# A two-column copy of a selective scan, moved from behind a table load to a place among the SiLUs

## The chip, the cores and the metric

The kernel runs on one core of one Trainium2 chip. The metric is the device time of one execution in microseconds (us). The engines are named as in the profile: PE (matrix multiplication), PEld (its weight loads), DVE (vector engine), ACT (activation engine), POOL (GpSimd), SP (the queue that issues most DMAs).

## What is computed

Two layers run over 32 images of 128 channels and 56 x 56 pixels. Layer 0 is a 7 x 7 depthwise convolution, a layer norm and a mixture of eight experts. Layer 1, in which the change lies, is a 1 x 1 convolution, a 3 x 3 convolution branch with SiLU, and a selective scan (Mamba) over the 3136 pixels of each image:

```python
xz = t @ in_proj_w.T
xm, z = jnp.split(xz, 2, axis=-1)              # 256 channels each
xm = silu(causal_conv4(xm) + conv1d_b)
dt, Bm, Cm = jnp.split(xm @ x_proj_w.T, [8, 24], axis=-1)
dt = softplus(dt @ dt_proj_w.T + dt_proj_b)
dA = exp(dt[..., None] * A)                    # 16 states for each channel
dBu = dt[..., None] * Bm[:, :, None, :] * xm[..., None]
h = dA_t * h + dBu_t                           # for every pixel in order
y = einsum('bds,bs->bd', h, C_t)
y = y + xm * D
return y * silu(z) @ out_proj_w.T
```

## The kernel before

Layer 1 cuts each image into 7 chunks of 448 pixels (8 rows). A chunk is called a group here; there are 32 x 7 = 224 groups, and each has 16 states. Channels lie on the 128 partitions, and the 256 channels of the scan are two halves side by side, so that one instruction on both halves has 2 x 448 columns, or 2 x 449 with a leading column for each half.

A unit u is one state i of one group: u = 16 g + i. For each unit

- POOL multiplies `db = du * B` (`db_pool`, L1099), with B copied to all partitions by a DMA from a small DRAM tile (`bc_load`, L1093);
- ACT computes the decay `da = exp(dt * A)` in two instructions, one for each half (`exp_act`, L1105). There are two `da` buffers, in PSUM, used by even and odd units in turn;
- DVE runs the scan `h = da * h + db` over 898 columns (`scan_dve`, L1114). In the leading column of each half the decay is zero and `db` holds the value that the state had at the end of the previous group, so one scan carries on both halves. For the states 0, 4, 6, 7, 12 and 15 (`POOL_C`) the result goes to a tile `hs` of its own; for the other ten it goes over `da` itself;
- POOL (for those six states) or DVE (for the ten) multiplies `prod = h * C` (`cmul`, L1120);
- ACT copies the two last values of `h`, one for each half, into the leading columns of that state's `db` tile (`carry_act`, L1126). In the last group of an image it copies zeros instead. The copy is next needed by the same state's scan one group later; and the decay of the unit two further on overwrites the `da` that it reads;
- PE sums `prod` over the states into the PSUM tile `py` (`sum_pe`, L1059).

The order of every engine's instructions is written out by hand in the loop at the end of `layer1`: step t issues the loads of units t+8 and t+4, `yz` if it falls in this step, POOL's product of unit t-1, the copy of unit t-1, `db` of unit t+4, the decay of unit t+1, the scan of unit t and, for the ten states, its product, then the sums and the side work. The side work of a group (`at(offset, function)`) is spread over the steps before and after its states.

In step i = 2 of each group the side work holds `silus(g)` of the following group. It works on ACT with another table of functions than the exponentials. In order: the table load of the SiLUs (L930), the two `xm` SiLUs (L930), the `lt` SiLU of the group before (L943), the two `zs` SiLUs (L946), and the table load of the exp set (L947). PE's two `p_z` products (L936), which the `zs` SiLUs read, go into the PSUM buffers that the `xm` SiLUs have read. `px_pe` (L953) follows on PE, then the `py` sums of step 3 and, in step 4, `p_cvc` (L829), which `sq_act` (L856) reads on ACT. `yz` (L1051) on DVE falls in step 4.

ACT's order around the SiLUs before the change is therefore: decay of state 3, table load, `xm`, `xm`, `lt`, `zs`, `zs`, table load, copy of state 2, decay of state 4, copy of state 3, decay of state 5.

Of the kernel before, what the change touches and what calls it, by code (L numbers as in the profile page):

```python
# [27 lines left out]
DS = 16  # L28
# [6 lines left out]
CH1 = L // NQ1  # L35
TPC1 = CH1 // TT
POOL_C = (0, 4, 6, 7, 12, 15)
HD = 64

NB0 = 4  # L40
# [4 lines left out]
def tile_kernel(tc: tile.TileContext, a: dict, out: bass.AP):  # L45
# [14 lines left out]
    with (  # L60
# [414 lines left out]
        def weights(wp, wt, pw):  # L475
# [13 lines left out]
            def turned(v, t):  # L489

                for h in range(2):
                    nc.sync.dma_start(
                        out=t[h * HD : (h + 1) * HD],
                        in_=v[h * 128 : (h + 1) * 128].rearrange("(r d) k -> d r k", r=2),
# [31 lines left out]
            for k in range(2):  # L526
                for r in range(2):
                    for j, v in enumerate((bbi, bsc)):
                        nc.scalar.copy(bnt[k * HD : (k + 1) * HD, r, j : j + 1], v[r * HD : (r + 1) * HD, :])

# [220 lines left out]
        with tc.tile_pool(name="p3", bufs=2, space=PSUM) as pmm:  # L751

            def mm_tile(name):
                return pmm.tile([128, 512], F32, name=name, tag="mm")

            layer1(w3 | locals())
# [3 lines left out]
def layer1(s):  # L760
# [12 lines left out]
    with (  # L773
# [149 lines left out]
        def silus(g):  # L923

            if g < G:
                d = st[g]
                xm = d["xm"] = two.tile([128, 2, CH1], F32, name="xm")
                zs = d["zs"] = three.tile([128, 2, CH1], F32, name="zs")
                for h in range(2):
                    nc.scalar.activation(  # L930
                        xm[:, h, :], d.pop(f"p_xm{h}")[:, :CH1], AF.Silu, bias=s["c1b"][:, h : h + 1]
                    )
                ps = []
                for h in range(2):
                    p = mm_tile("p_z")
                    nc.tensor.matmul(  # L936
                        p[:, :CH1], lhsT=s["wz"][:, h * 128 : (h + 1) * 128], rhs=d["te"][:, DC - 1 :],
                        start=True, stop=True,
                    )
                    ps.append(p)  # L940
            if g > 0:
                lt = st[g - 1]["lt"]
                nc.scalar.activation(lt, lt, AF.Silu)  # L943
            if g < G:
                for h in range(2):
                    nc.scalar.activation(zs[:, h, :], ps[h][:, :CH1], AF.Silu, bias=s["zb"][:, h : h + 1])  # L946
            nc.scalar.preload_act_table_set("natural_log_exp_and_others")  # L947
# [71 lines left out]
        def lt_pe(g, ts):  # L1019
# [5 lines left out]
            for t in ts:  # L1025
                dy, dx = divmod(t, 3)
                for r in range(2):
                    rs = slice(r * HD, (r + 1) * HD)
                    for k in range(2):
                        nc.tensor.matmul(  # L1030
                            d["p_l"][r][k * HD : (k + 1) * HD, : CH1 // 2], lhsT=s["dwd"][rs, t, rs],
                            rhs=d["xh"][rs, dy + k * R : dy + (k + 1) * R, dx : dx + HW], start=t == 0, stop=t == 8,
                        )

        def lt_act(g, r):
# [3 lines left out]
            lt, p = d["lt"], d["p_l"][r]  # L1039
            rs = slice(r * HD, (r + 1) * HD)  # L1040
            for k in range(2):
                ks = slice(k * HD, (k + 1) * HD)
                nc.scalar.activation(
# [23 lines left out]
        def dd_pe(g):  # L1067
            d = st[g]
            d["py"] = pyp.tile([128, 2, 512], F32, name="py3")
            tiles(py(g), lambda rs, h: s["dd"][rs, h, rs], d["xm"], True, False)  # L1070
# [17 lines left out]
        def bc_load(u, which):  # L1088
            g, i = divmod(u, DS)
            if i % SB == 0:  # L1090
                t = three.tile([128, SB, CH1], F32, name=which)
                r = DR + i + (DS if which == "cb" else 0)
                nc.sync.dma_start(out=t, in_=st[g]["bc_d"][r : r + SB, :].partition_broadcast(128))  # L1093
                for k in range(SB):
                    units[u + k][which] = t[:, k, :].unsqueeze(1).to_broadcast([128, 2, CH1])

        def db_pool(u):
            g, i = divmod(u, DS)
            nc.gpsimd.tensor_tensor(dbv[i][:, :, 1:], st[g]["du"], units[u].pop("bb"), ALU.mult)  # L1099

        def exp_act(u):
            g, i = divmod(u, DS)
            da = das[u % 2]
            for h in range(2):
                nc.scalar.activation(  # L1105
                    da[:, h * W1 : (h + 1) * W1], st[g]["dt"][:, h, :], AF.Exp, scale=s["aneg"][:, h, i : i + 1]
                )

        def scan_dve(u):
            i = u % DS  # L1110
            w = units[u]
            da = das[u % 2]
            hs = three.tile([128, 2 * W1], F32, name="hs", bufs=2) if i in POOL_C else da
            nc.vector.tensor_tensor_scan(hs, da, dbs[i], 0.0, ALU.mult, ALU.add)  # L1114
            w["hs"] = hs.rearrange("p (h t) -> p h t", h=2)

        def cmul(u, eng):
            w = units[u]
            w["prod"] = three.tile([128, 2, CH1], F32, name="prod", bufs=5)
            eng.tensor_tensor(w["prod"], w["hs"][:, :, 1:], w.pop("cb"), ALU.mult)  # L1120

        def carry_act(u):
            g, i = divmod(u, DS)
            hs = units[u].pop("hs")
            last = zeros if g % NQ1 == NQ1 - 1 else hs[:, :, CH1]
            nc.scalar.copy(dbv[i][:, :, 0], last)  # L1126

        def sum_pe(u):
            g, i = divmod(u, DS)
            tiles(py(g), lambda rs, h: ident[rs, rs], units[u].pop("prod"), False, i == DS - 1)  # L1130
# [29 lines left out]
        at(-33, moe_act)  # L1160
        at(-16, xm_pe, 1)
        at(-14, silus)
        at(-14, px_pe)
        at(-29, cv1_pe, "p_cvc", "cv1c")
# [10 lines left out]
        at(-25, var_pe)  # L1175
        at(-9, sp_exp)
        work.setdefault(DS * G - 14, []).append((silus, G))

        def valid(u):
            return 0 <= u < U  # L1180

        with tc.manual_schedule():
            for t in range(-40, U + 24):
                i = t % DS

                if valid(t + 8):
                    bc_load(t + 8, "bb")
                if valid(t + 4):
                    bc_load(t + 4, "cb")
                side = work.pop(t, [])  # L1190
                for w in side:
                    if w[0] is yz_dve:
                        w[0](*w[1:])

                if valid(t - 1) and (t - 1) % DS in POOL_C:
                    cmul(t - 1, nc.gpsimd)
                if valid(t - 1):
                    carry_act(t - 1)
                if valid(t + 4):
                    db_pool(t + 4)  # L1200

                if valid(t + 1):
                    exp_act(t + 1)

                if valid(t):
                    scan_dve(t)
                    if i not in POOL_C:
                        cmul(t, nc.vector)

                if i == 3 and valid(t - 3):  # L1210
                    dd_pe((t - 3) // DS)
                if i % 2 == 1:
                    for u in (t - 3, t - 2):
                        if valid(u):
                            sum_pe(u)
                for w in side:
                    if w[0] is not yz_dve:
                        w[0](*w[1:])
# [35 lines left out]
```

## Time and profile before

| What | Value |
|---|---|
| Median of 3 runs | 16215.65 us (16211.88 to 16220.98) |
| The profiled execution | 16201.56 us |
| Its span, first to last instruction | 16199.8 us |
| Granted PE clock, mean over the span | 0.907 |
| Busy share of PE, PEld, DVE, ACT, POOL over the span | 79%, 43%, 68%, 66%, 84% |
| The same from 5750 to 16150 us (layer 1) | 90%, 41%, 93%, 85%, 95% |
| Table load (L930, L947), each | 1.283 us |
| Decay (L1105), one half | 0.639 us |
| Scan (L1114) | 2.02 us |
| Copy (L1126) from `da`, from `hs` | 0.162 us, 0.193 us |

A line of the timeline gives the start in us, the duration in us, the engine, the line of the kernel and the operation, output before input, with the number of instructions merged into it; in brackets stands the idle time before it and what ended it. A line of the costliest groups gives after the bar the busy time in us, the mean duration in ns, the idle time in front of these instructions and, with an arrow, what ended most of it. The busy shares are averages over stages; what bounds a stage is read from the waits in it.

### The profile page before, as it was taken

Reading aid. Unit: us, or ns where it says so; the run is one execution under the profiler, and the core shown is the slowest. Engines: PE = TensorE matmul, PEld = TensorE weight load, DVE = VectorE, ACT = ScalarE, POOL = GpSimd, SP = SyncE. Lnnn points to the kernel's source line nnn. Section 1 sums busy time; section 2 is a strip of 40 time slices with the busy share of each in tenths; the row PEclk is TensorE's granted clock in tenths of the full one; section 3 lists DMA queues with packets and bytes.
Section 4 is the critical chain, followed back from the end, with each engine's and each line's share of the span. In section 5 each row is a group of like instructions: output and inputs, shape, how many; then the busy total and the mean of one; then the engine's idle time right before and its main releaser. Section 6 shows DMA issues by size and latency. Waiting matters only on the chain. (4 is left out here: it accounts for less than half of the span.)

```text
span 16199.8 us, 246168 instructions
## 1 busy us (share of the span) xinstructions
PE 12759.5 (79%) x91637; PEld 7021.4 (43%) x91637; DVE 11083.8 (68%) x9909; ACT 10643.5 (66%) x20982; POOL 13611.7 (84%) x9017
## 2 busy tenths in 40 slices
PE   7996100006999989999999999899899999999988
PEld 7995100005777734444444444444444444444443
DVE  2656300001111179999999999999999999999999
ACT  4655100003444478888888888888888888888887
POOL 2443477777888889999999999999999999999999
PEclk9996555558999999999999999999999999999999
DMA  8785433334555555555555555555555555555555
GB/s 266 231 240 195 158 105 102 107 96 69 71 71 72 64 154 175 172 175 176 173 176 174 175 176 174 174 175 175 174 173 175 175 173 176 175 174 175 175 173 162
DMA packets 1239122, 2572.09 MB, mean 159 GB/s; under 512 B 139336, under 2 KB 676640, under 8 KB 1230240
## 3 DMA queue, kind: packets, MB, share of 16 engines
q1 hardware_dynamic: 1041440, 2361.89, 47.1%
q0 software_dynamic: 196480, 194.45, 7.0%
q8 instruction: 721, 11.81, 0.3%
q14 instruction: 481, 3.94, 0.1%
HBM read 2180.38 MB, written 375.43 MB: 158 GB/s over the span
## 5 line engine op out<-in xcount | busy, mean ns | idle before, releaser
L1099 POOL TENSOR_TENSOR db<-du,bb 128x896 f32<-128x896 f32 x3584 | 6847.2, 1934 | 17.6
L1105 ACT ACTIVATE da<-dt,aneg 128x449 f32<-128x449 f32 x7168 | 4577.3, 639 | 269.4 <-DVE prod L1120 86.7
L1114 DVE TENSOR_TENSOR_SCAN da<-da,db 128x898 f32<-128x898 f32 x2240 | 4523.0, 2019 | 2.8 <-ACT da L1105 2.5
L1059 PE MATMUL py<-prod,ident 64*64 64x448 f32 x28672 | 3100.6, 545 | 21.7 <-POOL prod L1120 15.5
L1114 DVE TENSOR_TENSOR_SCAN hs<-da,db 128x898 f32<-128x898 f32 x1344 | 2673.1, 2015 | 487.4 <-ACT db L1126 441.9
L1120 POOL TENSOR_TENSOR prod<-hs,cb 128x896 f32<-128x896 f32 x1344 | 2595.1, 1931 | 459.8 <-PE p_cvc L829 343.6
L1120 DVE TENSOR_TENSOR prod<-da,cb 128x896 f32<-128x896 f32 x2240 | 2446.2, 1092 | 217.6 <-issue 3.5
L744 ACT COPY xc<-ept 128x512 f32<-128x512 f32 (+1 forms) x248 | 143.8, 580 | 2738.9 <-PE ept L742 2738.9
L650 POOL DMA_INDIRECT buf_d<-xg,slot x1568 | 1516.3, 967 | 487.3 <-issue 477.1
L702 POOL DMA_INDIRECT res_d<-ys,xb x984 | 1591.7, 1618 | 333.1 <-issue 285.6
L1059 PEld LDWEIGHTS py<-prod,ident 64*64 64x64 f32 x28672 | 1042.4, 133 | 1446.2 <-issue 1176.9
L742 PE MATMUL ept<-ident,xb 128*128 128x128 f32 (+1 forms) x984 | 188.8, 274 | 1849.0 <-DMA xb<-buf_d 1849.0
L914 PE MATMUL p_xm<-te,wk 128*128 128x448 f32 x3584 | 1415.8, 546 | 1.0 <-DVE te L898 0.6
L694 DVE TENSOR_TENSOR ys<-py,b2t 128x512 f32<-128x512 f32 (+2 forms) x256 | 170.9, 670 | 1679.4 <-PE py L688 1662.6
L647 DVE COPY xg<-gate 128x28 f32<-128x28 f32 x56 | 11.7, 213 | 1746.4 <-DMA buf_d<-xg,slot 1746.4
L688 PEld LDWEIGHTS py<-w2t,hh 128*128 128x128 f32 x7872 | 936.5, 191 | 175.2 <-issue 113.1
L688 PE MATMUL py<-w2t,hh 128*128 128x128 f32 x7872 | 985.2, 278 | 0.2
L914 PEld LDWEIGHTS p_xm<-te,wk 128*128 128x128 f32 x3584 | 658.7, 189 | 730.8 <-issue 572.0
L179 PE MATMUL pc<-xc,toep 112*112 112x112 f32 (+1 forms) x8192 | 935.0, 270 | 35.2 <-ACT toep L168 31.1
L742 PEld LDWEIGHTS ept<-ident,xb 128*128 128x128 f32 (+1 forms) x984 | 124.6, 143 | 1852.7 <-issue 1852.6
L179 PEld LDWEIGHTS pc<-xc,toep 112*112 112x112 f32 x8192 | 878.5, 184 | 45.3 <-ACT toep L168 38.8
L936 PE MATMUL p_z<-te,wz 128*128 128x448 f32 x896 | 522.3, 717 | 466.3 <-ACT xm L930 466.3
(235 smaller groups left out, 19412.9 us busy)
## 6 DMA issues: line engine op xcount, KB each, us to landing
bb<-bc_d SPq DMA_DIRECT2D x1792, 448.0 KB
cb<-bc_d SPq DMA_DIRECT2D x1792, 448.0 KB
toep<-toep_d SPq DMA_DIRECT2D x448, 392.0 KB
xg<-res_d SPq DMA_DIRECT2D x56, 1792.0 KB
buf_d<-zero SPq DMA_DIRECT2D x28, 2275.0 KB
xb<-buf_d SPq DMA_DIRECT2D x240, 260.0 KB
xt<-in_x SPq DMA_DIRECT2D x32, 1568.0 KB
res_d<-xa SPq DMA_DIRECT2D x128, 392.0 KB
```

What stands on the lines that cost most here:

```text
L179: nc.tensor.matmul(pc[:, c, :, lo:hi], lhsT=tp[c // 2][:, c % 2, 6 - 2 * o : 8 - 2 * o, :], rhs=s4[:, c, :, lo + o - 1 : hi + o - 1], star ...
L650: apart(nc.gpsimd.indirect_dma_start(out=buf_d[:, :], out_offset=bass.IndirectOffsetOnAxis(ap=slots[k][:, o + j : o + j + 1], axis=0), in_ ...
L688: nc.tensor.matmul(py[:n, j, :], lhsT=hh[:, k, j * 128 : j * 128 + n], rhs=w2t[:, k, :], start=k == 0, stop=k == KF - 1,)
L702: apart(nc.gpsimd.indirect_dma_start(out=res_d[:, :], out_offset=bass.IndirectOffsetOnAxis(ap=xb[:n, j, C + 1 : C + 2].bitcast(I32), axis= ...
L742: nc.tensor.transpose(pt[:, j * 128 : j * 128 + n], xb[:n, j, :C], ident[:n, :n])
L914: nc.tensor.matmul(p[:, :CH1], lhsT=s["wk"][:, k, hs], rhs=d["te"][:, k : k + CH1], start=k == 0, stop=k == DC - 1 and not first,)
L936: nc.tensor.matmul(p[:, :CH1], lhsT=s["wz"][:, h * 128 : (h + 1) * 128], rhs=d["te"][:, DC - 1 :], start=True, stop=True,)
L1059: nc.tensor.matmul(ps[r][h * HD : (h + 1) * HD, :CH1], lhsT=lhsT(rs, h), rhs=rhs[rs, h, :], start=start, stop=stop,)
L1099: nc.gpsimd.tensor_tensor(dbv[i][:, :, 1:], st[g]["du"], units[u].pop("bb"), ALU.mult)
L1105: nc.scalar.activation(da[:, h * W1 : (h + 1) * W1], st[g]["dt"][:, h, :], AF.Exp, scale=s["aneg"][:, h, i : i + 1])
L1114: nc.vector.tensor_tensor_scan(hs, da, dbs[i], 0.0, ALU.mult, ALU.add)
L1120: eng.tensor_tensor(w["prod"], w["hs"][:, :, 1:], w.pop("cb"), ALU.mult)
```

## The change

The copy of state 2 is no longer issued at the start of step 3, behind the second table load, but inside `silus`, behind the two `xm` SiLUs and PE's `p_z` products and ahead of the `lt` SiLU. There `g` is the following group, so `g - 1` is the group whose scan is running. The copies of the other 15 states stay where they are. In the built program the number of instructions and of table loads is the same, the order on PE, DVE, POOL and SP is the same, and ACT's order differs in this copy alone, once in each of the 224 groups.

```diff
@@ -35,6 +35,7 @@
 CH1 = L // NQ1
 TPC1 = CH1 // TT
 POOL_C = (0, 4, 6, 7, 12, 15)
+CARRY = 2
 HD = 64
 
 NB0 = 4
@@ -939,6 +940,7 @@
                     )
                     ps.append(p)
             if g > 0:
+                carry_act(DS * (g - 1) + CARRY)
                 lt = st[g - 1]["lt"]
                 nc.scalar.activation(lt, lt, AF.Silu)
             if g < G:
@@ -1194,7 +1196,7 @@
 
                 if valid(t - 1) and (t - 1) % DS in POOL_C:
                     cmul(t - 1, nc.gpsimd)
-                if valid(t - 1):
+                if valid(t - 1) and i != CARRY + 1:
                     carry_act(t - 1)
                 if valid(t + 4):
                     db_pool(t + 4)
```

## The prediction

> **What bounds the kernel now.** I read the slices of the page first: from slice 15 of 40 on, the busy digits no longer change, so layer 1 is a steady loop. Its 224 groups fill about 10,400 us (224 x 46.61, the mean distance from one group's first table load to the next in the timeline). Then the costliest groups of instructions and the list of waits, to see which engine of the loop ever stands still:
>
> ```profile
> L1114 DVE TENSOR_TENSOR_SCAN hs<-da,db 128x898 f32<-128x898 f32 x1344 | 2673.1, 2015 | 487.4 <-ACT db L1126 441.9
> L1120 POOL TENSOR_TENSOR prod<-hs,cb 128x896 f32<-128x896 f32 x1344 | 2595.1, 1931 | 459.8 <-PE p_cvc L829 343.6
> ...
> L936 PE MATMUL p_z<-te,wz 128*128 128x448 f32 x896 | 522.3, 717 | 466.3 <-ACT xm L930 466.3
> ```
>
> The reader is to see 487 us of idle DVE in front of one kind of scan, 460 us of idle POOL in front of one kind of product: about 2 us a group each, and no other large hole on either. Where the hole lies, the timeline of one group shows, ACT first, then DVE, then POOL:
>
> ```profile
> 10036.98 1.28 ACT L930 ACT_TABLE_LOAD   x1
> 10038.27 1.16 ACT L930 ACTIVATE xm<-p_xm,c1b 128x448 f32<-128x448 f32 x2
> 10039.32 0.58 ACT L943 ACTIVATE lt<-lt 128x448 f32<-128x448 f32 x1
> 10040.02 0.64 ACT L946 ACTIVATE zs<-p_z,zb 128x448 f32<-128x448 f32 x1
> 10041.15 0.63 ACT L946 ACTIVATE zs<-p_z,zb 128x448 f32<-128x448 f32 x1 [0.49 <-PE p_z L936]
> 10041.80 1.28 ACT L947 ACT_TABLE_LOAD   x1
> 10043.09 0.16 ACT L1126 COPY db<-da 128x2 f32<-128x2 f32 x1
> 10043.28 1.31 ACT L1105 ACTIVATE da<-dt,aneg 128x449 f32<-128x449 f32 x2
> ```
> ```profile
> 10035.34 2.02 DVE L1114 TENSOR_TENSOR_SCAN da<-da,db 128x898 f32<-128x898 f32 x1
> ...
> 10041.60 1.08 DVE L1051 TENSOR_TENSOR yz<-py,zs 128x896 f32<-128x896 f32 x1
> 10044.70 2.03 DVE L1114 TENSOR_TENSOR_SCAN hs<-da,db 128x898 f32<-128x898 f32 x1 [2.02 <-ACT db L1126]
> ```
> ```profile
> 10046.86 1.92 POOL L1120 TENSOR_TENSOR prod<-hs,cb 128x896 f32<-128x896 f32 x1 [1.82 <-PE py L1059]
> ```
>
> The DVE is done with yz at 10042.68 and waits for the decay of state 4, which ends on ACT at 10044.59; the scan starts 0.1 later, and POOL's product of state 4 follows that scan. ("PE py" is only the last releaser by the profile; the scan's end at 10046.73 is what came 0.13 before.) ACT is late because five SiLUs lie between two table loads, and the copy of state 2 stands after the second load. So once a group the loop hangs on the chain: DVE product of state 1, decay of state 3, load, SiLUs, load, copy, decay of state 4, scan of state 4. All else in the group is DVE work back to back. A tenth saved on this chain is a tenth off the group, as long as the hole (1.3 us in the shortest groups, 3.2 in the longest) is larger than that.
>
> **What the skill says.** "ScalarE: Activation LUTs", section "Table sets: the hidden batching unit": cheap functions, copy among them, are filler in every set, so a copy among SiLUs needs no load. The trace of before runs these copies with the exp set alone, so it can't show it; the built program after the change still has two loads a group. "Perfetto Trace Analysis", section "Per-instruction lifecycle": ACT is strictly first in, first out, and a wait for a semaphore lies before the reported start. The trace agrees: the decay stands 0.19 behind the copy at 10043.09, with nothing between. "TensorE: Matmul & The Clock Gate", Part 1: the array's clock is halved by a free-running window of 4096 cycles (3.413 us) after idling. The trace agrees: the stretches that begin with the wait for xm have a granted clock of 0.79 in some groups and 1.00 in others, and sorting the 223 first loads by start time modulo 3.413 us sorts the blocks into short and long ones.
>
> **The change, part by part.** Nothing is added: 224 copies leave the place after the second load and stand behind the xm SiLUs. Only ACT's order changes; no DMA, no matmul and no instruction of SP or POOL moves.
>
> *Removed after the load.* Between the load's end and the copy lie 0.01 us. In 192 groups the copy reads da, and the decay of state 4 overwrites da, so it waits for the copy: 0.195 us from start to start in each. In the other 32 (last of an image) it copies zeros and the decay follows 0.098 after it. Afterwards the decay follows the load at once; the SiLU behind the first load starts 0.01 after it (10038.26 to 10038.27), so I take the whole distance: 192 x 0.195 + 32 x 0.098 = 40.6 us. Bound below: if the decay, whose scale is a pointer, needs 0.1 more after a load, 40.6 - 22 = 18 us; above there is no more to take.
>
> *Added among the SiLUs.* The copy needs the scan of state 2. That ends at 10037.36; its new place is reached about 10039.32, where lt starts now. So it is 1.96 us in hand and nothing queued behind it (lt, two zs, load, decay) waits for DVE. A copy whose successor doesn't wait for it costs 0.08 to 0.1 (the copy at 10047.94 and the decay at 10048.02). lt then starts at about 10039.41, zs could start at 10039.9, but zs starts at 10040.02 because p_z is ready only then, and the second zs at 10041.15, after 0.49 of waiting. The cover is PE's p_z, which hangs on the xm SiLUs ahead of the copy and is not moved. Cost taken: 0. If that cover were gone it would cost 0.1 x 224 = 22 us.
>
> *What is late next.* PE's row is not moved: p_z, p_x, the py sums and p_cvc still follow xm. Thus ACT's square (L856), which already waits for p_cvc in 108 groups, waits as much longer as ACT comes earlier, and the decays of states 6 and 7 behind it don't move. In the quoted group the square waited 0.92, and the scans of states 6 and 7 took 4.18 us together instead of 3.94. Going through the timeline, the scan of state 7 has no slack once that wait is 0.69 or more (27 groups), and 0.21 when it is under 0.5. Lost: 27 x 0.19 + 15 groups between x 0.1 = 6.6 us. Left: 34 us, bounds 12 and 41.
>
> *The clock window.* A group's length depends on where its first load lies in the 3.413 us window:
>
> ```profile
> core 0: us, PE busy (x) PEld busy (x) DVE busy (x) ACT busy (x) POOL busy (x), PEclk, DMA share, GB/s
> 9336.11:9382.17 46.06, 41.15 (x306) 19.15 (x306) 43.47 (x29) 39.67 (x81) 44.27 (x28) 1.00 0.57 176
> 9382.17:9429.49 47.32, 42.65 (x306) 19.43 (x306) 43.46 (x29) 39.67 (x81) 44.62 (x28) 0.96 0.55 173
> ```
>
> Two neighbouring groups with the same work: the second is 1.26 us longer at a lower clock. Load to load takes 4.44 us in 97 groups (mean group 46.06), over 5.2 in 87 (47.20). A group of 46.06 advances by 46.06 - 13 x 3.413 = 1.69, half a window, so two bring the loop back almost to the same place. Starts are bunched: 113 of 223 lie in the three eighths of the window around its turn. If all eighths were equally frequent, the mean of the eighths' means would be 46.54, not 46.61: 0.07 x 223 = 16 us. A group of 45.87 advances by 1.50 and spreads the starts more evenly; I take 15 us more gain, an estimate, with bounds of a gain of 40 and a loss of 25, since the bunching can turn out either way.
>
> *Sum.* 40.6 - 6.6 + 15 = 49 us. The profiled execution took 16201.56 (span 16199.8), which would become about 16152.5; it lies 14 below the median of the three runs, 16215.65. On that median the forecast is 16215.65 - 49 = 16166.
>
> **The rivals.** *The late square takes most of it back*: if every one of the 108 groups that wait for p_cvc loses its part, 116 x 0.18 = 21 us remain and the clock gives nothing: 16195. For it: the wait grows by construction. Against: state 7 has slack in most of them. *The change does nothing*: the copy lengthens the SiLU block by what it frees behind it. if it takes 0.18 there as on average after the load, 40.6 - 40.3 = about 0, 16216. Against it: the 0.49 and 0.12 of waiting in front of the zs. *Slower by the clock window*: the new step bunches the groups in the long part. A long group costs 47.20 - 46.06 = 1.14 more than a short one, so 34 gained us are eaten by 30 more long groups (87 to 117), and from 60 more it is slower beyond the measurement; 70 more give 16215.65 - 34 + 80 = 16262. For it: the present bunching shows that the step can lock. Against: the present one is near a half window, the new one is not near a simple fraction.
>
> **How the numbers follow.** The measurement can tell about 0.2% (32 us) from no change. Forecast 0.77, at 16166, its own range 16130 to 16183; square takes it back 0.11 (16195); does nothing 0.06 (16216); slower 0.06 (16262). Faster by over 0.2%: 0.77; within: 0.11 + 0.06 = 0.17; slower: 0.06. The range runs from 16130 (41 direct and 40 of clock are 81, little beyond it) up to 16200, which takes in the second case and leaves out the last two, 0.12, and tails.
>
> **What would show it.** After: no copy at L1126's new number between the second load and the decay; the decay 0.01 behind the load; zs starting as long after xm as now (1.75 us in a short group), and load to load still 4.44 in short groups; shortest groups 45.87 instead of 46.06; DVE's idle before hs down from 487 to about 450 us; ACT's wait for p_cvc up from 61.5 by some 20 to 30 us. Wrong if lt or zs start later than p_z allows, if the short groups stay at 46.06, or if the share of groups over 5.2 us from load to load rises above half.

## The result, and the profile after

Six runs of the changed kernel gave a median of 16164.69 us (16146.63 to 16166.55), six of the kernel before 16218.31 (16209.85 to 16236.96): a ratio of 0.9965, 95% interval 0.9954 to 0.9976, or 54 us (39 to 75 by the interval). The forecast was 16166. The profiled execution took 16164.69 (span 16163.0), so the two profiles lie only 37 us apart; layer 1 accounts for more than that, as the row of the decays, which gives their number, their shortest, median and longest duration in ns and the start of the first and the last, shows for each kernel:

```profile
L1105 ACT ACTIVATE da<-dt,aneg x7168: 629/639/648, 5740.1 to 16183.2; 128x449 f32<-128x449 f32 x200
```
```profile
L1107 ACT ACTIVATE da<-dt,aneg x7168: 629/639/649, 5750.6 to 16146.6; 128x449 f32<-128x449 f32 x200
```

From first to last decay it is 10443.1 before and 10396.0 after, 47 us less. Layer 0, which the change doesn't touch, happened to end 10.5 later in the second profile. This length of layer 1 is what I compare below, beside the ratios. It is read from one trace of each kernel; two traces of the changed kernel differ by 3.5 us (10396.0 and, in `after_again`, 10392.5), and with fillers two of one kernel agree (10274.4 in `e_after_dummy` and in `e_again`).

The page of the changed kernel, its costliest groups (all line numbers have moved by one or two):

```profile
L1116 DVE TENSOR_TENSOR_SCAN hs<-da,db 128x898 f32<-128x898 f32 x1344 | 2674.9, 2015 | 437.5 <-ACT db L1128 387.6
L1122 POOL TENSOR_TENSOR prod<-hs,cb 128x896 f32<-128x896 f32 x1344 | 2599.2, 1934 | 404.7 <-PE p_cvc L830 234.2
...
L937 PE MATMUL p_z<-te,wz 128*128 128x448 f32 x896 | 505.9, 697 | 466.3 <-ACT xm L931 466.3
```

The busy times and durations of the scan and of POOL's product are nearly those of before, and p_z is a little faster (697 ns a matmul instead of 717). What shrank is the idle time before the scan, 487.4 to 437.5 (about 450 was forecast, without the clock's part), and before POOL's product, 459.8 to 404.7. The timeline of ACT in one group, and of DVE in the same stretch:

```profile
10034.20 1.28 ACT L931 ACT_TABLE_LOAD   x1
10035.49 1.16 ACT L931 ACTIVATE xm<-p_xm,c1b 128x448 f32<-128x448 f32 x2
10036.54 0.16 ACT L1128 COPY db<-da 128x2 f32<-128x2 f32 x1
10036.58 0.60 ACT L945 ACTIVATE lt<-lt 128x448 f32<-128x448 f32 x1
10037.24 0.64 ACT L948 ACTIVATE zs<-p_z,zb 128x448 f32<-128x448 f32 x1
10038.57 0.63 ACT L948 ACTIVATE zs<-p_z,zb 128x448 f32<-128x448 f32 x1 [0.69 <-PE p_z L937]
10039.22 1.28 ACT L949 ACT_TABLE_LOAD   x1
10040.51 1.31 ACT L1107 ACTIVATE da<-dt,aneg 128x449 f32<-128x449 f32 x2
...
10044.63 0.63 ACT L857 ACTIVATE sq<-p_cvc,cv1cb 128x448 f32<-128x448 f32 x1 [0.91 <-PE p_cvc L830]
```
```profile
10034.67 1.09 DVE L1122 TENSOR_TENSOR prod<-da,cb 128x896 f32<-128x896 f32 x1
10035.68 2.03 DVE L1116 TENSOR_TENSOR_SCAN da<-da,db 128x898 f32<-128x898 f32 x1
...
10041.93 2.03 DVE L1116 TENSOR_TENSOR_SCAN hs<-da,db 128x898 f32<-128x898 f32 x1 [2.03 <-ACT db L1128]
```

The decay of state 4 now follows the load at once (10039.22 + 1.28 to 10040.51). Summed over all groups, the time from the end of the second load to that decay falls from 43.0 to 2.7 us. The copy puts lt 0.04 us later than it would be, and the first zs starts 1.75 after the first xm as before. The number of table loads is 455 in both traces. The hole before the scan of state 4 is still there, 2.03 us in this group; its length goes with the time from the start of the first table load to that of the second, called load to load below.

### The profile page after: what moved, and what is told of

Read it like the earlier page. It is cut to its first block, busy times and chain, and to the rows that moved or that the text cites. A ratio compares the mean times of both kernels' runs of the same rounds, so it can differ in the third digit from the quotient of the medians.

```text
span 16163.0 us, 246168 instructions
## 1 busy us (share of the span) xinstructions
PE 12742.0 (79%) x91637; PEld 7006.1 (43%) x91637; DVE 11083.6 (69%) x9909; ACT 10626.3 (66%) x20982; POOL 13620.3 (84%) x9017
## 5 line engine op out<-in xcount | busy, mean ns | idle before, releaser
L1116 DVE TENSOR_TENSOR_SCAN hs<-da,db 128x898 f32<-128x898 f32 x1344 | 2674.9, 2015 | 437.5 <-ACT db L1128 387.6
L1122 POOL TENSOR_TENSOR prod<-hs,cb 128x896 f32<-128x896 f32 x1344 | 2599.2, 1934 | 404.7 <-PE p_cvc L830 234.2
L651 POOL DMA_INDIRECT buf_d<-xg,slot x1568 | 1517.1, 968 | 487.4 <-issue 477.1
L210 POOL TENSOR_TENSOR xa<-xa,lng 112x896 f32<-112x896 f32 x128 | 267.3, 2089 | 745.9 <-ACT xa L207 685.3
```

The lines of the kernel that those rows point to most:

```text
L210: nc.gpsimd.tensor_tensor(xa, xa, lng.unsqueeze(1).to_broadcast([TT, w, C]), ALU.mult)
L651: apart(nc.gpsimd.indirect_dma_start(out=buf_d[:, :], out_offset=bass.IndirectOffsetOnAxis(ap=slots[k][:, o + j : o + j + 1], axis=0), in_ ...
```

## The experiments

`after_again`, `h_two_fill`, `f_before_dummy` and `i_sq_later` ran on a chip on which the kernel before takes 16219.67 us. The other eight ran on one with about 16410, nearly all of the difference in layer 0. Each ratio is to the kernel before on the same chip.

**The changed kernel once more** (`after_again`, no edit).

> The changed kernel once more, as a mark for the other kernels beside it. The same ratio to the kernel before as at first, 0.9965 (0.995 to 0.998).

Measured: 0.9961 (0.9947 to 0.9974), 16158.02 us. The result repeats.

**Fillers on PE** (`e_after_dummy`, again as `e_again`): what is added in `silus`, ahead of the loop over p_z; `yz_was` holds the last yz tile.

```diff
+                if g > 2:
+                    old = st[g - 3].pop("yz_was")
+                    for k in range(4):
+                        nc.tensor.matmul(
+                            st[g - 2]["py"][:, k % 2, CH1:512], lhsT=ident, rhs=old[:, k % 2, : 512 - CH1],
+                            start=True, stop=True,
+                        )
```

> The changed kernel with four small matmuls of 64 columns added on PE in every group from the third on, between the py sums and p_z, into columns of the py tile that nothing reads. Theory (long groups come from PE's clock, halved after PE idled while waiting for xm): with the idle time filled the p_z matmuls run at full clock, load to load is near 4.44 us in most groups, mean group 46.40 down to 45.9 to 46.1, 16055 to 16100. Rival 1 (p_z is late for another reason, the fillers only queue ahead of it): 16165 to 16230. Rival 2 (the fillers are too small to count as activity): 16165 within 10, p_z as slow as before.

> The changed kernel with four fillers once more, as the mark for the three beside it, where the clock window no longer blurs small differences. Ratio to the kernel before 0.9889 again (0.988 to 0.990), about 16040 if this chip is as fast as the last.

Measured: 0.9889 (0.9874 to 0.9905) and 0.9896 (0.9881 to 0.9911). Adding work to PE made the kernel 0.7% faster than the changed one. The groups of `e_again`:

```profile
L944 PE MATMUL p_z<-te,wz 128*128 128x448 f32 x896 | 399.5, 568 | 237.3 <-ACT xm L931 237.3
```

p_z takes 568 ns a matmul instead of 697, and PE waits 237 us for xm instead of 466. Stretches of one group each, first of the changed kernel, then of `e_again`; the columns are the stretch, its length, the busy time of PE, PEld, DVE, ACT and POOL with the number of instructions, the granted PE clock, the DMA share and GB/s:

```profile
10173.61:10219.47 45.86, 41.07 (x306) 19.11 (x306) 43.46 (x29) 39.58 (x81) 44.29 (x29) 1.00 0.56 178
10219.47:10266.65 47.18, 42.73 (x306) 20.13 (x310) 43.28 (x29) 39.32 (x79) 44.19 (x29) 0.96 0.54 171
10266.65:10312.51 45.86, 41.77 (x316) 19.03 (x306) 43.66 (x29) 39.21 (x80) 44.58 (x28) 1.00 0.56 178
```
```profile
10175.83:10221.69 45.86, 42.10 (x317) 20.08 (x315) 43.46 (x29) 39.59 (x80) 44.28 (x28) 1.00 0.54 176
10221.69:10267.56 45.87, 42.12 (x317) 20.11 (x315) 43.48 (x29) 39.60 (x81) 44.34 (x28) 1.00 0.51 178
10267.56:10313.42 45.86, 42.10 (x317) 20.10 (x315) 43.46 (x29) 39.59 (x81) 44.30 (x28) 1.00 0.54 176
```

In the changed kernel a group of 47.18 us at clock 0.96 stands between two of 45.86 at 1.00; with fillers all three are 45.86 or 45.87. Going through the starts of the loads in the timeline, load to load is 4.44 us in 220 of 224 groups, where it was in 97 before and in 106 after the change. So the long groups come from PE's clock, as the Trainium skill ("TensorE: Matmul & The Clock Gate", Part 1) lets one expect: keep PE from idling, and they are gone. The page has the clock low after an idle window of about 3.4 us; here a wait of 2.2 us is enough in many groups, and the measurement decides. Which groups are long goes with the start. Sorted by start modulo 3.4134 us, the value near the page's 3413 ns that sorts the changed kernel's loads best, load to load is 4.44 in all 80 groups of seven neighbouring sixteenths of the window, and from there its median climbs to 6.02.

**Two fillers** (`h_two_fill`, on the changed kernel with fillers).

```diff
-                    for k in range(4):
+                    for k in range(2):
```

> The changed kernel with two fillers instead of four. Theory (what counts is how long PE idles within the clock's window): the idle time of about 2.2 us shrinks by half as much, so some groups stay long, between the changed kernel (0.9965) and four fillers (0.9889), about 0.992. Rival (any filler is enough): 0.989. Rival (a threshold is missed): 0.9965.

Measured: 0.9955 (0.9941 to 0.9968), 6.6 us below `after_again`, which the intervals don't separate.

```profile
L944 PE MATMUL p_z<-te,wz 128*128 128x448 f32 x896 | 504.9, 697 | 336.6 <-ACT xm L931 336.6
```

By its mean, p_z is as slow as without fillers, as the rival with a threshold has it. But the mean mixes two kinds of groups. Load to load is 4.44 us in 128 groups here (106 and 110 in the two traces of the changed kernel) and over 5.2 in 87 (74 and 71): fewer groups are slowed, and those more. Layer 1, 10382.0 (5756.6 to 16138.6), is 10 to 14 us shorter than without fillers. So the theory's "between" isn't refuted, and the mean alone doesn't show a threshold; the counts by length of the wait, in the last section, tell more.

**The kernel before with four fillers** (`f_before_dummy`: the lines added for the fillers above, in the kernel before).

> The kernel before with the same four small matmuls ahead of p_z as in the changed kernel with fillers. Theory (the change is worth 0.195 us in 192 groups and 0.098 in 32, 40.6 us, and the rest of the measured gain is the clock window): with the window out of play the gap to the changed kernel with fillers is 40.6 us and no more; ratio to the kernel before 0.9914 where the changed kernel with fillers has 0.9889; short groups 46.06, and most groups short. Rival (the whole 54 us are the copy's own, by work it frees elsewhere): the gap is 54 us, ratio 0.992. Second rival (the fillers help for another reason than the clock): load to load stays spread.

Measured: 0.9914 (0.9901 to 0.9928), 16082.14 us, as the theory has it; that the last digit agrees is chance with this interval. Its row of decays and that of `e_again`:

```profile
L1112 ACT ACTIVATE da<-dt,aneg x7168: 629/639/650, 5749.6 to 16064.4; 128x449 f32<-128x449 f32 x200
```
```profile
L1114 ACT ACTIVATE da<-dt,aneg x7168: 628/639/649, 5944.9 to 16219.3; 128x449 f32<-128x449 f32 x200
```

Layer 1 takes 10314.8 and 10274.4: 40.4 us apart, where 40.6 were worked out. With the clock out of play this is the change's own worth. The loss at the square is gone too: it still waits for p_cvc in 222 groups of `e_again`, mostly for 0.29 us, but no wait is long enough to hold up the scan of state 7 (the gaps ahead of it add up to 0.7 us). The wait, with its total, number and longest in us:

```profile
ACT sq L857 <- PE p_cvc L830: 76.1, 222, 2.0
```

**The copy made twice** (`g_both`, with four fillers: among the SiLUs and again behind the load).

```diff
-            hs = units[u].pop("hs")
+            hs = units[u]["hs"]
...
-                if valid(t - 1) and i != CARRY + 1:
+                if valid(t - 1):
```

> With four fillers, and the copy made twice, among the SiLUs and once more behind the second load, where it stood. Theory (the only price is that the decay of state 4 waits for a copy behind the load): as the kernel before with fillers, 192 x 0.195 + 32 x 0.098 = 41 us slower than the changed kernel with fillers, ratio about 0.9914. Rival (part of the gain comes from the copy's being early, or from a lighter row of ACT): well below 41 us.

Measured: 0.9918 (0.9904 to 0.9931), 34 us above `e_again` in the medians; layer 1 takes 10314.4, 40.0 more than `e_again` (in the medians part of that is hidden by a layer 0 that ended 14 us earlier in the trace of this one).

```profile
L1114 ACT ACTIVATE da<-dt,aneg x7168: 628/639/649, 5930.9 to 16245.3; 128x449 f32<-128x449 f32 x200
```

The copy behind the load costs the whole 40 us whether or not it has been made earlier. Nothing else of the move can be told from zero here.

**No copy of state 2** (`d_no_copy` and, with fillers, `d_fill`).

```diff
             if g > 0:
-                carry_act(DS * (g - 1) + CARRY)
                 lt = st[g - 1]["lt"]
```

> The copy of state 2 is left out in every group, so state 2 starts each group from zero: part of the computation is missing. Theory (the moved copy costs nothing): the same as the changed kernel, 16165 within 8. Rival (the moved copy still lengthens the block by 0.04 to 0.1 us a group): 9 to 22 us faster, 16143 to 16156.

> With four fillers, and the copy of state 2 left out in every group (state 2 starts each group from zero: part of the computation is missing). Theory (the copy ahead of lt is free): the same as with it, within 4 us. Rival (it costs its 0.04 us by which lt is later): 9 us faster.

Measured: 0.9961 (0.9947 to 0.9975) beside 0.9965 and 0.9961 for the changed kernel, and 0.9898 (0.9882 to 0.9913) beside 0.9896, with 16233.69 against 16233.58 us. Layer 1 takes 10276.2 against 10274.4 with fillers, and 10392.3 against 10396.0 and 10392.5 without. In its new place the copy costs nothing that can be measured, and there is no more to be had from its place.

**Behind the zs SiLUs** (`a_before_load` and, with fillers, `a_fill`): the copy in `silus` stands just ahead of the second load.

```diff
             if g > 0:
-                carry_act(DS * (g - 1) + CARRY)
                 lt = st[g - 1]["lt"]
...
+            if g > 0:
+                carry_act(DS * (g - 1) + CARRY)
             nc.scalar.preload_act_table_set("natural_log_exp_and_others")
```

> The copy stands behind both zs SiLUs and ahead of the second table load. Theory (the copy is free where it is because ACT waits there for p_z anyway; behind the second zs nothing is waited for): the load starts 0.06 to 0.08 us later in every group, the decay still follows the load at once, 224 x 0.07 = 16 us slower than the changed kernel, about 16181 (16172 to 16195). Rival 1 (only leaving the place behind the load counts): as the changed kernel, 16165. Rival 2 (the copy costs the same anywhere on ACT's row): as before, 16216.

> With four fillers, the copy behind both zs SiLUs and ahead of the second load. Theory: 0.05 us a group, as the load then starts 4.494 instead of 4.443 us behind the first, 11 us slower than the changed kernel with fillers. Rival (any place ahead of the load is free): the same within 4 us.

Measured without fillers: 0.9966 (0.9952 to 0.9979), 4.5 us above `d_no_copy` on the same chip: inconclusive, below both the 16 expected and what the intervals separate; layer 1, 10403.0, is 10.7 above `d_no_copy`. With fillers: 0.9902 (0.9887 to 0.9918), 16245.74, 12.2 us above `e_again` where 11 were expected; layer 1 takes 10289.6, 15.2 more, of which 14 lie in load to load (4.538 in the mean instead of 4.474). So three places cost 0 (ahead of lt), 12 to 15 (ahead of the load) and 40 us (behind it): the wait for p_z is the cover, and behind the second zs there is none.

**Ahead of the first load** (`c_first`).

```diff
         def silus(g):
 
+            if g > 0:
+                carry_act(DS * (g - 1) + CARRY)
             if g < G:
```

> The copy stands ahead of the first table load, where the scan of state 2 is not done: it ends 0.38 us behind the present start of the load. Theory (ACT works strictly in order, and the copy's free place depends on its 1.96 us in hand): the load waits for the scan and the copy, 0.38 + 0.13 + 0.16 = 0.67 us later in each group, 224 x 0.67 = 150 us slower than the changed kernel, about 16315 (16280 to 16360), with an ACT wait for the scan in front of each such copy. Rival (the scan is early enough or the block has slack): 16165 to 16216.

Measured: 1.0303 (1.0287 to 1.0319), about 560 us above `d_no_copy` on the same chip, which stands for the changed kernel there; 150 were expected. Its timeline on ACT, that on DVE, and the row of p_z:

```profile
10062.37 1.31 ACT L1108 ACTIVATE da<-dt,aneg 128x449 f32<-128x449 f32 x2
10065.30 0.16 ACT L1129 COPY db<-da 128x2 f32<-128x2 f32 x1 [1.62 <-DVE prod L1123]
10065.48 1.28 ACT L933 ACT_TABLE_LOAD   x1
```
```profile
10062.06 2.03 DVE L1117 TENSOR_TENSOR_SCAN da<-da,db 128x898 f32<-128x898 f32 x1
10064.17 1.09 DVE L1123 TENSOR_TENSOR prod<-da,cb 128x896 f32<-128x896 f32 x1
```
```profile
L939 PE MATMUL p_z<-te,wz 128*128 128x448 f32 x896 | 678.3, 907 | 834.7 <-ACT xm L933 834.7
```

The bracket names what I had overlooked: the copy waits for the product of state 2, not for its scan. The scan ends at 10064.09, the product at 10065.26, and the copy starts at 10065.30; in 191 groups it starts within 0.06 us of the product's end. So the load starts 2.44 us after the start of the decay's second half instead of 0.66, and 1.48 after it in the 31 groups whose copy is of zeros: 191 x 1.78 + 31 x 0.82 = 365 us. The rest is the clock: PE now waits 4.0 us for xm in those 191 groups, p_z takes 907 ns in the mean, and load to load is 5.72 us in the mean instead of 4.95, 0.77 x 224 = 172. The sum, 537, is near the 553 by which layer 1 is longer than the changed kernel's (10948.9 against 10396.0).

**The square one step later** (`i_sq_later`).

```diff
-        at(-28, sq_act)
-        at(-28, cv1_pe, "p_cv1", "cv1t")
+        at(-27, sq_act)
+        at(-27, cv1_pe, "p_cv1", "cv1t")
```

> The changed kernel with the square and its p_cv1 product one step later, so that ACT does the copy of state 4 and the decay of state 6 before it waits for p_cvc. Theory (the change lost 6 to 8 us where the square, held by p_cvc, makes the decay of state 7 late): ACT's wait for p_cvc falls from 107 us to under 20, the scan of state 7 waits no more, 8 to 14 us faster than the changed kernel, ratio to before about 0.996. Rival (the later square makes p_cv1 and the work behind it late): the same or slower than the changed kernel.

Measured: 0.9977 (0.9969 to 0.9985), 16182.6 us, 25 above `after_again`: slower, as the rival has it. The waits of the changed kernel, then those of this one, each with total, number and longest in us:

```profile
ACT sq L857 <- PE p_cvc L830: 106.9, 201, 2.0
```
```profile
DVE da L1116 <- ACT da L1107: 15.9, 29, 1.3
...
ACT sq L857 <- PE p_cvc L830: 2.0, 1, 2.0
```

The square waits no more, and in the timeline the gaps ahead of the scan of state 7 fall from 12.9 us in `after_again` to 0.6. But the work behind the later square makes the decay of state 11 late (the scans over da wait 15.9 us for it; 2.7 in the changed kernel), and that takes back what the square gives: outside load to load a group takes 41.45 us in the mean in both kernels. The 17 us by which layer 1 is longer than in `after_again` (10409.3 against 10392.5) lie in load to load, 5.006 in the mean instead of 4.937 and over 5.2 us in 84 groups instead of 71. That part goes with PE's clock (p_z takes 713 ns a matmul instead of 694), and the gaps in front of the scans don't account for it. So the run doesn't tell what the later square is worth by itself; with fillers it was not run.

## Why the prediction was right, and where its steps were off

*Removed after the load: right.* 40.6 us were forecast. The time from load to decay shrank by 40.3, and `f_before_dummy` and `g_both` measure 40.4 and 40.0 of layer 1.

*Added among the SiLUs: right in the sum, wrong in a reason.* The cost of nothing holds (`d_fill`). The copy puts lt off by 0.04 us and not by 0.08 to 0.1. But the hand was mis-sized: "1.96 us in hand" counted from the scan's end, and the copy waits for the product. In the quoted group of before that ends at 10038.54, so 0.8 us were in hand:

```profile
10037.45 1.09 DVE L1120 TENSOR_TENSOR prod<-da,cb 128x896 f32<-128x896 f32 x1
```

That this was enough is luck, as far as the reasoning goes; `c_first` shows what it costs when it is not. The list of waits of before had it: ACT's copies are held up 701 times by "DVE prod".

*What is late next: right in the loss; the wait that was to show it was taken too small.* A loss of 6.6 us at state 7 was forecast. Summed over the timeline, the gaps ahead of that scan, counted above the shortest one, are 6.0 us before and 13.6 after, 7.6 more. ACT's wait for p_cvc, though, rose by 45 us (61.5 to 106.9) and not by 20 to 30: groups that had not waited do so now, 201 instead of 108. Most of that wait falls where nobody is held up by it. The line of before, beside that of the changed kernel above:

```profile
ACT sq L856 <- PE p_cvc L829: 61.5, 108, 2.0
```

*The clock window: right in size, not shown in its reason.* A gain of 15 us was taken, with anything from a loss of 25 to a gain of 40 held possible, so that it came out is in part luck. Mean load to load fell from 5.021 to 4.950 us, 16 us over 224 groups; and 47.1 of layer 1, less 40.6, plus 7.6, leaves 14. That the long groups are the clock's is shown by the fillers, and there are fewer of them (over 5.2 us: 87 before, 74 and 71 in two profiles after). That the new length of a group spreads the starts more evenly over the window is not shown. Sorted into eighths as in the prediction, the mean group lies 0.07 us above that of even starts before and 0.02 and 0.01 in the two profiles after. But it lies 0.10 above in `d_no_copy`, whose short groups have the same length and whose layer 1 is as short. The cause of this part stays open.

*The sum.* 49 us were forecast and 54 measured, which the interval makes 39 to 75; that 16166 and 16164.69 lie so close is chance.

*The rivals.* "The change does nothing" falls with `f_before_dummy` and `d_fill`, "the late square takes most of it back" with the 7.6 us, and "slower by the clock window" with the counts, though `c_first` shows that the clock can take 172 us in this loop.

The fastest version tried is the changed kernel with four fillers, about 1.1% below the kernel before. What remains is the hole before state 4, some 320 us in all (321.8 idle before hs in `e_again`), which two table loads and five SiLUs make.

## What to carry to other kernels

Price a small instruction on an engine that works in order by what stands behind it: 0.16 us of copying cost 0.195 us a group where the next instruction had to wait for it, and nothing where the engine was about to wait for another anyway. Before a step is put earlier, read from the brackets which instruction released it so far; the data it reads may be ready while its semaphore is not. In this loop, where PE waits about two us each time round, part of a change of length can be the clock's doing; fillers in that wait took it out and made differences of 10 us readable.

## What the runs showed of the hardware

How often p_z is slow depends on how long PE has waited before it. Its four matmuls take 1.77 us together in a group where nothing slows them; counted in the timeline, a group is called slow here when they take over 1.9. After a wait under 1.3 us none of 213 groups is slow (`e_again`), after 1.5 to 1.8 us 92 of 183 (`h_two_fill`), after 2.15 to 2.7 us 116 of 190 (`after`), and after more than 3.5 us all 191 (`c_first`). In between, 8 groups of `e_again` waited 1.3 to 1.5 us, and 3 of them are slow. So in this loop the slowing sets in between 1.3 and 1.5 us, as far as so few groups can tell, well under the 3.41 us of the window, and a longer wait makes it more frequent. A mean hides this: p_z has 697 ns a matmul both with two fillers (95 slow groups) and with none (117).
